# A Mamba, cross-attention and mixture-of-experts decoder on one core: opening, passage to the experts and last norm in another order

## The chip, the core and the metric

The kernel runs on one core of a Trainium2 chip. The time is device microseconds of one execution, and the figure for the kernel before is a median of 3 runs. All arithmetic is float32.

A core has five engines that run their own instruction queues and meet through semaphores: TensorE (PE in the profile; its weight loads are PEld), VectorE (DVE), ScalarE (ACT), GpSimd (POOL) and SyncE (SP). SP only issues DMAs; ACT and POOL issue some of theirs.

## The reference, cut to what matters

Three blocks, each followed by a layernorm: a Mamba layer, an attention over a second sequence, and a mixture of 32 experts with one shared expert. Batch B = 8, length S = 512, width D = 512, inner width 1024, state 16, 16 heads of 32, 4 of 32 experts for each token, capacity 640 rows for each expert.

```python
# Mamba
xz = _layernorm(x, ln_w, ln_b) @ in_proj_w
x_main, z = jnp.split(xz, 2, axis=-1)
x_main = jax.nn.silu(conv1d_causal(x_main) + conv_b)            # 4 taps along the sequence
dt, B_ssm, C_ssm = jnp.split(x_main @ x_proj_w, [DT_RANK, DT_RANK + D_STATE], axis=-1)
dt = jax.nn.softplus(dt @ dt_proj_w + dt_proj_b)
h = dA_t * h + dBx_t                                            # dA = exp(-exp(A_log) * dt), dBx = dt * B * x_main
y_t = jnp.einsum('bdn,bn->bd', h, C_t)                          # for every t of 512
x = _layernorm(x + (res_scale * ((y + x_main * D_param) * jax.nn.silu(z)) @ out_proj_w + x))
# attention over ctx
x = _layernorm(x + softmax(where(mask, q @ k.T / sqrt(32), -1e8)) @ v @ Wo.T + bo)
# experts
scores = softmax(xf @ wg.T)                                     # 8 groups of 4; the best 4 groups, then the best 4 experts
w, idx = top_k(masked, 4);  w = w / (w.sum() + 1e-9)
pos = (jnp.cumsum(oh, axis=0) * oh).sum(-1) - 1;  keep = pos < cap
dest = jnp.where(keep, fe * cap + pos, E * cap)                 # row of the token in its expert's buffer
h = silu(xe @ w1) * (xe @ w3);  out = (h @ w2) * buf_w
y = zeros.at[buf_tok].add(out)
z = silu(xf @ sw1) * (xf @ sw3) @ sw2
out = _layernorm(x + y + z)
```

## The kernel before

The program is three functions, run one after another: `layers()` (Mamba and attention with the gate and the shared expert), `experts()` and `finish()` (the last layernorm). Pools hand out the tiles; a scheduler of the framework may move an instruction within its engine's queue as far as dependencies allow, so the order in the source isn't exactly that on the engines. Line numbers are those of the kernel before.

**Opening of `layers()`.** `const` (L128) allocates a tile and loads it with a DMA on SP. It is called for the layernorm's and convolution's weights, then 16 DMAs bring A_log into `aneg` (L149), ScalarE takes its Exp and VectorE its negative (L153, L154), then come bq, bk, bv, bo and wg, masks and counters on GpSimd, the mask (L217 to L221) which is made into fill values and sent to `filld` in memory, and the load of Wo with four products (L974 to L978) that fold bv through Wo into bo. Only then `load_x` (L272) loads the first 256 rows of x, and `pieces()` (L263) issues the first weights of the Mamba projections. `pieces()` is a generator: it issues one load ahead of the one that it returns, and the tiles `wm` have three buffers.

**First chunk.** `norm_x` computes the layernorm (L54 to L79), `flip_x` transposes (L287), and `convolve` (L303 the projection, L323 the copy, L329 the first tap, L337 the other three) runs for four groups q of 256 channels; each fetches its piece. The tile `xp` has a single buffer. Then `silu` (L354), `x_proj` with `spill` (L360 to L368: B and C go to memory as `scr`), `prepare` (dt for one q: L390 to L413, spread over the partitions by 4 DMAs each for dt and dtx, L419), `bcast` (one group of B and C broadcast from memory, L379) and `decays` (the exponentials with `aneg`, L438).

**The loop.** There are 16 chunks (8 images of two halves of 256 positions), each of 32 steps over (q, g, ci): channel group, group of 4 states, channel block. A step makes h's input (L450), scans (L454), multiplies by C (L471) and sums over states on TensorE (L475). `settle()`, `do()` and `dry()` are a list of deferred second halves: `do` starts a piece of work and leaves its remainder to the next call; `dry` finishes all. Side work is woven into the steps by weights: `sources(0)` in the first image, later `units(b - 1)`, the attention and shared expert of the image before. After the loop, `units(B - 1)` runs alone: flips of x1 (L734), queries (L704 and L743), scores (L767), maxima (L769), and so on to the second layernorm. In chunks 0 and 1, every odd step clears the rows of one expert in the buffer `xbuf` (L237, 1.36 MB).

**Passage to the experts.** The end of `units` is a list built by `add(weight, function)`: transpose x2 (L870), sw1 in four parts, with `pick` (logits L540, the gate L547 to L603) after its first; sw3 in four parts, with `place` (L615 to L636: the position of each token in its expert, counted by matmuls, to `dest`) after the fourth, and after the third for the last image; then 16 `send`s (L642: GpSimd's indirect DMAs that scatter rows to `xbuf`) and the second matmul of the shared expert.

**Pools.** The Mamba tiles lie in the pools `p1`, `p2` and `p3` beside those of the attention; the experts' pools are allocated after `layers()`, and each is tied to the release of what had the space.

**`experts()`.** `load(e)` issues on SP the rows of one expert, `xe` (L1136), and its w1, w3, w2 (L1139, 1 MB each; two buffers), then TensorE flips xe (L1171), VectorE sums weights (L1162: sums of halves of the weights, which take part in the products), and TensorE runs `hidden` (L1200) and the product with w2. GpSimd adds the results into `based` (L1280).

**`finish()`** goes through 8 pieces of 512 rows: load acc on SP (L1367), layernorm on VectorE and ScalarE (helper lines L54 to L79: statistics, Ln and Exp for the root, `m` by five small operations, then four rows o on ScalarE), and a store issued by ScalarE (L1370). acc and o have four buffers each.

Of the kernel before, what the change touches and what calls it, by code (L numbers as in the profile page):

```python
# [1 line left out]

# [5 lines left out]
F32 = mybir.dt.float32  # L8
# [8 lines left out]
P = 128  # L17
# [9 lines left out]
T = 256  # L27
# [54 lines left out]
def layers(ctx, tc, a, x1d, filld, based, xbuf):  # L82
# [23 lines left out]
    nc = tc.nc  # L106
    cp = ctx.enter_context(tc.tile_pool(name="l_const", bufs=1))
# [5 lines left out]
    bcp = ctx.enter_context(tc.tile_pool(name="l_bc", bufs=6))  # L113
# [19 lines left out]

    lnw = const("lnw", [P, DC], a["ln_w"])
# [18 lines left out]
    nc.scalar.activation(aneg, aneg, AF.Exp)  # L153
    nc.vector.tensor_scalar(aneg, aneg, -1.0, None, ALU.mult)  # L154
# [6 lines left out]
    das = [cp.tile([P, NG, T + 1], F32, name=f"l_da{i}") for i in range(2)]  # L161
    for da in das:
        nc.gpsimd.memset(da[:, :, 0:1], 0.0)

    bq = const("bq", [P, DC], a["bq"])
    nc.vector.tensor_scalar(bq, bq, HD**-0.5, None, ALU.mult)
    bk = const("bk", [P, DC], a["bk"])
    bv = const("bv", [P, DC], a["bv"].rearrange("(c p) -> p c", p=P))
    bo = const("bo", [P, D], a["bo"].partition_broadcast(P))
    wg = const("wg", [P, DC, E], rows(a["wg"]))  # L170
# [44 lines left out]

    mu8 = p3.tile([P, D], F32, tag="row", name="mu8").bitcast(U8)[0:B, 0:S]
    nc.sync.dma_start(mu8, a["mask"])  # L217
    fl = p3.tile([P, D], F32, tag="row", name="fl")
    nc.vector.tensor_copy(fl[0:B, :], mu8)
    nc.vector.tensor_scalar(fl[0:B, :], fl[0:B, :], -1.0, 1e8, ALU.add, ALU.mult)  # L220
    nc.sync.dma_start(filld, fl[0:B, :])  # L221

# [21 lines left out]
    def pieces():  # L244


        w_in, w_out = rows(a["in_proj_w"]), rows(a["out_proj_w"])
        xs = [w_in[:, :, 2 * q * P : 2 * (q + 1) * P] for q in range(CC // 2)]
        zs = [w_in[:, :, DI + 2 * q * P : DI + 2 * (q + 1) * P] for q in range(CC // 2)]
        outs = [w_out[:, 2 * q : 2 * q + 2, :] for q in range(CC // 2)]  # L250
        n = B * (S // T)
        order = list(xs)
        for i in range(n):
            order += (outs if i else []) + zs + (xs if i + 1 < n else [])
        order += outs
        got = None
        for src in order + [None]:
            nxt = None
            if src is not None:
                nxt = p2.tile([P, 4 * 2 * P], F32, tag="wm", name="wm", bufs=3).rearrange(  # L260
                    "p (c f) -> p c f", c=src.shape[1]
                )
                nc.sync.dma_start(nxt, src)  # L263
            if got is not None:
                yield got
            got = nxt

    piece = pieces()

    def load_x(b, t, f):  # L270
        f["xt"] = xt = p1.tile([P, NT_, D], F32, tag="xt", name="xt")
        nc.sync.dma_start(xt, a["x"][b, t * T : (t + 1) * T, :].rearrange("(j p) d -> p j d", p=P))  # L272
# [6 lines left out]
    def flip_x(q, f):  # L279
        if q == 0:  # L280
            f["xnT"], f["xs"] = p1.tile([P, DC, T], F32, tag="xnT", name="xnT"), {}
# [30 lines left out]
    def convolve(t, q, f):  # L312
# [4 lines left out]
        def first_tap():  # L317
            xp = p1.tile([P, 2, T + 3], F32, tag="xp", name="xp")
# [7 lines left out]
            f["xs"][q] = xs = p2.tile([P, 2, T], F32, tag="xs", name="xs", bufs=5)  # L326
# [18 lines left out]
    def gate_x(q, f):  # L345
        if q == 0:
            f["zs"] = p1.tile([P, CC, T], F32, tag="zs", name="zs")
        ps = project(f, "ps_z")
        return lambda: nc.scalar.copy(f["zs"][:, 2 * q : 2 * q + 2, :], ps) and None
# [7 lines left out]
    def x_proj(f):  # L357
# [6 lines left out]
        def spill():  # L364
            f["xd"] = xd = p1.tile([64, T], F32, tag="xd", name="xd")
# [19 lines left out]
    def prepare(q, f):  # L385
# [8 lines left out]
        def exponentials():  # L394
            u = p1.tile([P, 2, T], F32, tag="u", name="u")
            dt = p1.tile([P, 2, T], F32, tag="dt", name="dt")
# [6 lines left out]
            l = p1.tile([P, 2, T + 3], F32, tag="xp", name="l")[:, :, 0:T]  # L403
            nc.scalar.activation(l, u, AF.Ln, bias=1.0)
            w = dtx = p1.tile([P, 2, T], F32, tag="dtx", name="dtx")
            nc.scalar.activation(w, u, AF.Identity, bias=1.0)

            def both():
# [6 lines left out]
                for src in (dt, dtx):  # L415
                    to = p2.tile([P, 2, 2, T], F32, tag=f"both{len(f['ready', q])}", name="both")
# [23 lines left out]
    def carry(t, c, g):  # L440

        last = state[:, c, g].unsqueeze(2)
        h = p3.tile([P, NG, T + 1], F32, tag="h", name="h", bufs=4)
# [45 lines left out]
    def twice_x(b, t, f):  # L489
        f["o"] = o = p1.tile([P, NT_, D], F32, tag="xt", name="o")  # L490
# [216 lines left out]
    def units(b):  # L707
# [241 lines left out]
        for j in range(SC):  # L949
            add(0.5, flip2, j, dry=(j == 0))  # L950
        for ic in range(DC):
            add(3.4, hidden, "sw1", ic, dry=(ic == 0))
            if ic == 0:
                add(1.5, lambda: pick(b, st["x2t"], st["x2T"], st))
        for ic in range(DC):
            add(3.4, hidden, "sw3", ic)
            if ic == (2 if b == B - 1 else 3):
                add(0.5, lambda: place(*st["picked"], st))
        sends = [(0, send, j, st) for j in range(SC)]
        if b == B - 1:  # L960
            for part in sends:
                add(*part)
# [5 lines left out]


    load("Wo")  # L970
    rep = p3.tile([P, D], F32, tag="row", name="rep")
    psb = psm.tile([P, D], F32, tag="mm", name="ps_bo")
    for dc in range(DC):
        nc.vector.tensor_copy(rep[:, dc * P : (dc + 1) * P], bv[:, dc : dc + 1].to_broadcast([P, P]))  # L974
        nc.tensor.matmul(
            psb, rep[:, dc * P : (dc + 1) * P], loaded["Wo"][:, dc, :], start=(dc == 0), stop=(dc == DC - 1)
        )
# [442 lines left out]
```

## Time and profile before

| | |
|---|---|
| time, median of 3 runs | 5591.53 us (5585.55 to 5597.78) |
| the profiled execution: its time | 5587.21 us |
| its span on the core | 5585.2 us |
| TensorE busy | 4864.8 us, 87% |
| VectorE busy | 4348.3 us, 78% |
| ScalarE busy | 2589.2 us, 46% |
| GpSimd busy | 565.5 us, 10% |
| mean granted TensorE clock | 0.938 |
| DMA | 769.83 MB, mean 138 GB/s |
| x issued by SP | 26.14 us |
| first product of the scan loop on VectorE | 81.87 us |
| first flips of the last image | 3746.32 us |
| first flips of the first expert | 3969.45 us |
| first statistics of the last norm | 5533.36 us |

The profiled execution is 4.3 us faster than the median. Times in the timelines count from the start of its span. A row has the start, the length, the engine (SPq, ACTq are queues that issue DMAs), the line, the operation, output and inputs by the program's names, and the number of instructions joined in the row; the bracket holds the idle time of the engine before it and what ended that. The rows by stretch give each engine's busy time (and number of instructions), the granted clock of TensorE, the mean busy share of the 16 DMA engines and their rate. The clock is granted in tenths of full speed and says nothing of whether TensorE was busy.

### The profile page before, as it was taken

The page shows a single profiled execution, that of the slowest core. Times are in us where ns is not written, and L with a number is a line of the kernel's source. Part 1 is how long each engine was busy: PE and PEld are TensorE (multiplying, and loading weights), DVE is VectorE, ACT ScalarE, POOL GpSimd, SP SyncE. Part 2 cuts the span into 40 slices and gives each one's busy share as a digit, 9 for nine tenths or more (in the row PEclk, how much of TensorE's full clock was granted, in tenths as well). Part 3 has the DMA queues.
Part 4 walks back from the last instruction along what each step waited for, and adds up shares of the span by engine and source line. Part 5 has one row for each costly group of instructions (what it writes and reads, how often), then busy time and mean ns, then how long its engine had stood idle before and what let it go on. Part 6 is the DMA issues. An engine that isn't in the chain of part 4 may idle for free. (4 is left out here: it accounts for less than half of the span.)

```text
span 5585.2 us, 60354 instructions
## 1 busy us (share of the span) xinstructions
PE 4864.8 (87%) x19752; PEld 2711.8 (49%) x19752; DVE 4348.3 (78%) x5738; ACT 2589.2 (46%) x5481; POOL 565.5 (10%) x424
## 2 busy tenths in 40 slices
PE   5667888888988988888888898889899999999994
PEld 3233344334433434443443343333577777777773
DVE  5998999999889999898989999853566565555554
ACT  4554655565566555565555656523222222222223
POOL 0000002001100200200010020010111111111111
PEclk8778999999999999999999999989999999999997
DMA  7787345444634634543463464431445545454444
GB/s 202 214 230 203 106 130 183 123 115 134 187 105 112 199 103 127 180 129 109 128 199 101 116 189 111 113 118 37 140 124 126 125 125 125 119 126 125 123 115 139
DMA packets 560426, 769.83 MB, mean 138 GB/s; under 512 B 135754, under 2 KB 268394, under 8 KB 560112
## 3 DMA queue, kind: packets, MB, share of 16 engines
q1 hardware_dynamic: 522608, 680.70, 41.6%
q0 software_dynamic: 33280, 76.90, 7.3%
q10 hardware_dynamic: 4224, 8.39, 0.4%
q8 instruction: 156, 2.56, 0.2%
q14 instruction: 158, 1.29, 0.1%
HBM read 508.68 MB, written 165.05 MB: 121 GB/s over the span
## 5 line engine op out<-in xcount | busy, mean ns | idle before, releaser
L438 ACT ACTIVATE l_da<-both,l_aneg 128x256 f32<-128x256 f32 x2048 | 889.1, 499 | 816.9 <-DVE h L454 775.4
L454 DVE TENSOR_TENSOR_SCAN h<-l_da,h 128x1028 f32<-128x1028 f32 x512 | 1169.8, 2292 | 51.6 <-ACT h L444 29.6
L475 PE MATMUL py<-h,l_twice 128*64 128x256 f32 x4096 | 625.4, 419 | 210.5 <-DVE h L471 210.3
L450 DVE TENSOR_TENSOR h<-both,bc 128x1024 f32<-128x1024 f32 x512 | 617.8, 1214 | 134.4 <-PE py L475 72.0
L471 DVE TENSOR_TENSOR h<-h,bc 128x1024 f32<-128x1024 f32 x512 | 622.4, 1218 | 8.2 <-DMA bc<-scr 2.1
L475 PEld LDWEIGHTS py<-h,l_twice 128*64 128x64 f32 x4096 | 292.5, 146 | 585.9 <-DVE h L471 251.0
L767 PE MATMUL ps_s<-l_ka,l_qa 64*128 64x512 f32 x1024 | 319.3, 703 | 141.7 <-DVE mx L769 141.3
L1200 PE MATMUL ps_h<-xT,w 128*128 128x320 f32 x1536 | 436.1, 434 | 0.0
L1280 POOL DMA_INDIRECT based<-y,xe x160 | 252.2, 1577 | 1314.3 <-ACT y L1303 573.8
L769 DVE TENSOR_REDUCE mx<-ps_s 128x2 f32<-128x1024 f32 x256 | 310.1, 1214 | 82.7 <-PE ps_s L767 81.8
L1221 DVE TENSOR_TENSOR hT<-ps_h,p 128x320 f32<-128x320 f32 x128 | 62.9, 491 | 374.9 <-PE ps_h L1200 374.7
L1200 PEld LDWEIGHTS ps_h<-xT,w 128*128 128x128 f32 x1536 | 292.5, 191 | 118.4 <-issue 0.8
L793 PE MATMUL ps_t<-l_qa,l_ka 64*128 64x512 f32 x1024 | 298.0, 646 | 15.8 <-ACT eT L797 12.1
L797 ACT ACTIVATE eT<-ps_t 128x1024 f32<-128x1024 f32 x256 | 258.7, 1012 | 109.5 <-PE ps_t L793 109.3
L809 PE MATMUL po<-eT,l_va 128*64 128x512 f32 x1024 | 279.2, 623 | 24.4 <-ACT raw L821 19.6
L1200 PE MATMUL ps_h<-t,s 128*128 128x320 f32 x1024 | 286.1, 432 | 0.0
L642 POOL DMA_INDIRECT xbuf<-x2t,dest x128 | 218.3, 1706 | 651.2 <-DVE dest L636 561.8
L704 PE MATMUL ps_p<-x2T,wa 128*128 128x512 f32 x512 | 245.5, 629 | 12.9 <-DVE hT L884 10.7
L303 PE MATMUL ps_z<-xnT,wm 128*128 128x256 f32 x1024 | 240.9, 388 | 15.4 <-DVE o L513 13.0
L303 PE MATMUL ps_x<-xnT,wm 128*128 128x256 f32 x1024 | 240.8, 389 | 3.2 <-ACT dt L401 1.9
L504 PE MATMUL po<-wm,zs 128*128 128x512 f32 x512 | 233.3, 605 | 3.3 <-DMA wm<-in_out_proj_w 1.8
L1200 PEld LDWEIGHTS ps_h<-t,s 128*128 128x128 f32 x1024 | 194.6, 190 | 81.1
(225 smaller groups left out, 7401.3 us busy)
## 6 DMA issues: line engine op xcount, KB each, us to landing
bc<-scr SPq DMA_DIRECT2D x1024, 128.0 KB
w<-in_w SPq DMA_DIRECT2D x96, 1024.0 KB
wm<-in_in_proj_w SPq DMA_DIRECT2D x128, 512.0 KB
xbuf<-zero SPq DMA_DIRECT2D x32, 1362.5 KB
xe<-xbuf SPq DMA_DIRECT2D x32, 1362.5 KB
both<-dt SPq DMA_DIRECT2D x256, 128.0 KB
both<-dtx SPq DMA_DIRECT2D x256, 128.0 KB
wm<-in_out_proj_w SPq DMA_DIRECT2D x64, 512.0 KB
```

Of the source, the lines that this page charges most:

```text
L303: nc.tensor.matmul(ps[:, i, :], w[:, dc, i * P : (i + 1) * P], f["xnT"][:, dc, :], start=(dc == 0), stop=(dc == DC - 1),)
L438: nc.scalar.activation(da[:, n, 1:], dt[:, c % 2, j, :], AF.Exp, scale=aneg[:, c, j, g, m : m + 1])
L450: nc.vector.tensor_tensor(steps, dtx[:, c % 2].unsqueeze(2).to_broadcast([P, 2, NG // 2, T]), bc[0], ALU.mult)
L454: nc.vector.tensor_tensor_scan(flat, da.rearrange("p n t -> p (n t)"), flat, 0.0, ALU.mult, ALU.add)
L471: nc.vector.tensor_tensor(steps, steps, bc[1], ALU.mult)
L475: nc.tensor.matmul(py[j * HP : (j + 1) * HP, c % 2, :], twice, h[:, j * 2 + m, 1:], start=False, stop=(s == (NST // NG - 1, NG // 2 - 1, 1)),)
L767: nc.tensor.matmul(ps[:, j, :], qa[r, lt * P : (lt + 1) * P], ka[r, :], start=True, stop=True)
L769: return lambda: nc.vector.tensor_reduce(mx[:, lt, :].unsqueeze(2), ps, AX.X, ALU.max) and None
L793: nc.tensor.matmul(ps[:, j, :], ka[r, kc * P : (kc + 1) * P], qa[r, :], start=True, stop=True)
L797: nc.scalar.activation(eT, ps, AF.Exp)
L809: nc.tensor.matmul(po[j * 2 * HD : (j + 1) * 2 * HD, :], va[:, kc, i, j * HD : (j + 2) * HD], eT[:, j, :], start=(kc == 0), stop=(kc == SC ...
L1200: nc.tensor.matmul(ps, w[:, n, r * P : (r + 1) * P], x[:, n, :], start=not more and n == 0, stop=n == 1, skip_group_check=more,)
```

## The change

It is in six parts, and leaves the arithmetic of every one of them as it was.

- x's first rows are loaded by SP's first instruction, and two pieces of Mamba's weights are started ahead of the constants (`begun`). Aneg's Exp and sign move to just before the first `decays`.
- The bias work (scale of bq, the mask's fill values, Wo and bo) moves into a function, called in the steps k = 0 (load of Wo) and k = 2 of the first chunk; the scheduler places it early in them.
- The clears of chunks 0 and 1 follow a count spread over the 64 steps from step 6 on, in place of every odd step.
- The Mamba tiles go into a pool of their own, `l_mamba`, allocated first together with the pool of bc, so that the experts' constants and weights take the space that it frees. The weights of expert 0 are issued by ACT.
- For the last image only, `pick` comes ahead of sw1, `place` after the first part of sw3, and the sends after the second part.
- `finish` starts the statistics of piece i before it completes piece i − 1, and maps rows as "(p j) d", so that a partition holds 4 rows that follow each other in memory (8 KB in one) instead of 4 separate rows of 2 KB.

The diff, cut:

```diff
+    mp = ctx.enter_context(tc.tile_pool(name="l_mamba", bufs=1))
+    bcp = ctx.enter_context(tc.tile_pool(name="l_bc", bufs=6))
     cp = ctx.enter_context(tc.tile_pool(name="l_const", bufs=1))
...
-    bcp = ctx.enter_context(tc.tile_pool(name="l_bc", bufs=6))
...
+    def begun(it):
+        first = next(it)
+        return chain([first], it)
+
+    x0 = p1.tile([P, NT_, D], F32, tag="xt", name="xt")
+    nc.sync.dma_start(x0, a["x"][0, 0:T, :].rearrange("(j p) d -> p j d", p=P))
+    piece = begun(pieces())
     lnw = const("lnw", [P, DC], a["ln_w"])
...
-    nc.scalar.activation(aneg, aneg, AF.Exp)
-    nc.vector.tensor_scalar(aneg, aneg, -1.0, None, ALU.mult)
+    bq = const("bq", [P, DC], a["bq"])
...
-    bq = const("bq", [P, DC], a["bq"])
-    nc.vector.tensor_scalar(bq, bq, HD**-0.5, None, ALU.mult)
...
-    mu8 = p3.tile([P, D], F32, tag="row", name="mu8").bitcast(U8)[0:B, 0:S]
-    nc.sync.dma_start(mu8, a["mask"])
...
-    nc.sync.dma_start(filld, fl[0:B, :])
...
-    piece = pieces()
...
-        f["xt"] = xt = p1.tile([P, NT_, D], F32, tag="xt", name="xt")
+        f["xt"] = xt = mp.tile([P, NT_, D], F32, tag="xt", name="xt")
...
+        end = b == B - 1
+        if end:
+            add(1.5, lambda: pick(b, st["x2t"], st["x2T"], st), dry=True)
+        sends = [(0, send, j, st) for j in range(SC)]
         for ic in range(DC):
             add(3.4, hidden, "sw1", ic, dry=(ic == 0))
-            if ic == 0:
+            if ic == 0 and not end:
                 add(1.5, lambda: pick(b, st["x2t"], st["x2T"], st))
         for ic in range(DC):
             add(3.4, hidden, "sw3", ic)
-            if ic == (2 if b == B - 1 else 3):
+            if ic == (0 if end else 3):
                 add(0.5, lambda: place(*st["picked"], st))
-        sends = [(0, send, j, st) for j in range(SC)]
-        if b == B - 1:
-            for part in sends:
-                add(*part)
+            if ic == 1 and end:
+                for part in sends:
+                    add(*part)
...
-    f = {}
-    load_x(0, 0, f)
+    f = {"xt": x0}
...
     bc, n = bcast(f, 0), 0
+    nc.scalar.activation(aneg, aneg, AF.Exp)
+    nc.vector.tensor_scalar(aneg, aneg, -1.0, None, ALU.mult)
     decays(0, 0, f["ready", 0][0], das[0])
...
+            if i == 0 and k == 0:
+                load("Wo")
+            if i == 0 and k == 2:
+                biases()
...
-            if i < 2 and k % 2:
-                clear(i * E // 2 + k // 2)
+            while i < 2 and cleared < E * (i * len(steps) + k - 6) // (2 * len(steps) - 7):
+                clear(cleared)
+                cleared += 1
...
+        start = nc.sync.dma_start if e else nc.scalar.dma_start
         nc.sync.dma_start(xe, xbuf[e * CAP : (e + 1) * CAP, :].rearrange("(j p) d -> p j d", p=P))
         for n in ("w1", "w3", "w2"):
             got[n] = w = wp.tile([P, DC, D], F32, tag=n, name=n)
-            nc.sync.dma_start(w, a[n][e].rearrange("(c p) f -> p c f", p=P))
+            start(w, a[n][e].rearrange("(c p) f -> p c f", p=P))
...
+    def sums(i):
         rows = slice(i * S, (i + 1) * S)
         acc = pp.tile([P, SC, D], F32, tag="acc", name="acc")
-        nc.sync.dma_start(acc, based[rows, :].rearrange("(j p) d -> p j d", p=P))
+        nc.sync.dma_start(acc, based[rows, :].rearrange("(p j) d -> p j d", j=SC))
...
+            nc.vector.bn_stats(st, acc[:, j, :])
+            nc.vector.bn_aggr(mv[:, j, :], st)
...
+        nc.scalar.activation(r, v, AF.Ln)
+        nc.scalar.activation(r, r, AF.Exp, scale=-0.5)
+        return rows, acc, mv, v, r
...
+    def end(rows, acc, mv, v, r):
...
+        for j in range(SC):
+            nc.scalar.activation(o[:, j, :], acc[:, j, :], AF.Identity, bias=m[:, j : j + 1], scale=r[:, j : j + 1])
+        nc.scalar.dma_start(out[rows, :].rearrange("(p j) d -> p j d", j=SC), o)
...
+    for i in range(B):
+        now = sums(i)
+        if last:
+            end(*last)
+        last = now
+    end(*last)
```

`biases()` holds the lines that were at L166, L217 to L221 and L975 to L978 unchanged; in `finish`, `end(*last)` holds the five small operations of the helper and the four rows on ScalarE. All other tiles of the Mamba chunk (`wm`, `xnT`, `xp`, `xs`, `zs`, `xd`, `u`, `dt`, `l`, `dtx`, `both`, `h`, `l_da`, `o`) move to `mp` with the number of buffers that they had.

## The prediction

> **What bounds the kernel now.** I read the page's busy shares and slices first (TensorE 87% busy over the whole span, VectorE 78%), then busy time by stretch, then the timelines of the stretches where neither engine works.
>
> ```profile
> start us, us, engine line op out<-in xcount [idle before <-releaser]
> 26.14 0.39 SPq L272 DMA_DIRECT2D xt<-in_x  x1
> ...
> 31.79 1.29 DVE L73 BATCH_NORM_STATS2 st<-xt 128x6 f32<-128x512 f32 x2 [5.49 <-DMA xt<-in_x]
> ...
> 81.87 2.36 DVE L450 TENSOR_TENSOR h<-both,bc 128x1024 f32<-128x1024 f32 x2 [8.16 <-DMA bc<-scr]
> ```
>
> Opening: SP sends x at 26.14, behind every constant; the first work of the scan loop is at 81.87.
>
> ```profile
> core 0: us, PE busy (x) PEld busy (x) DVE busy (x) ACT busy (x) POOL busy (x), PEclk, DMA share, GB/s
> 82.00:300.00 218.00, 145.82 (x614) 76.39 (x615) 209.77 (x213) 114.75 (x275) 12.90 (x4) 0.80 0.73 210
> 3739.00:3766.00 27.00, 19.01 (x44) 8.86 (x46) 0.13 (x1) 5.25 (x8) 0.13 (x1) 0.75 0.24 73
> 3950.00:3976.00 26.00, 4.20 (x16) 3.03 (x17) 6.19 (x10) 0.00 (x0) 6.14 (x7) 0.54 0.77 284
> 4100.00:5508.00 1408.00, 1407.98 (x5764) 1040.86 (x5762) 827.49 (x1487) 389.71 (x851) 231.99 (x147) 1.00 0.48 118
> 5540.00:5545.00 5.00, 0.00 (x0) 0.00 (x0) 4.96 (x15) 2.66 (x7) 0.00 (x0) 0.50 0.30 61
> ```
>
> The loop is VectorE's (209.77 of 218); in the experts TensorE never pauses. Time can therefore come only from the seams: to 82, at 3739 to 3766, at 3950 to 3976, and after 5523. The last image:
>
> ```profile
> 3746.32 1.94 PE L734 MATMUL ps_tr<-l_ident,xr 128*128 128x128 f32 x8 [9.13 <-DMA xr<-x1d]
> ...
> 3766.60 3.68 DVE L769 TENSOR_REDUCE mx<-ps_s 128x2 f32<-128x1024 f32 x3 [27.46 <-PE ps_s L767]
> ...
> 3909.28 0.29 DVE L547 TENSOR_REDUCE g_m<-ps_l 128x4 f32<-128x128 f32 x1 [15.49 <-PE ps_l L540]
> ...
> 3929.76 0.39 PE L615 MATMUL ps_b<-g_any,l_before 128*128 128x128 f32 x2
> ...
> 3956.99 0.97 POOL L642 DMA_INDIRECT xbuf<-x2t,dest  x1 [0.30 <-issue]
> ...
> 3969.45 1.09 PE L1171 MATMUL ps_t<-e_ident,xe 128*128 128x128 f32 x4 [21.31 <-DMA xe<-xbuf]
> ```
>
> and the finish:
>
> ```profile
> 5527.88 27.58 SPq L1367 DMA_DIRECT2D acc<-based  x8
> 5533.36 1.29 DVE L73 BATCH_NORM_STATS2 st<-acc 128x6 f32<-128x512 f32 x2 [26.28 <-DMA acc<-based]
> ...
> 5545.43 0.15 DVE L59 TENSOR_TENSOR m<-v,r 128x4 f32<-128x4 f32 x1
> ...
> 5580.15 0.38 ACTq L1370 DMA_DIRECT2D out<-o  x1
> ```
>
> Read the bracket as the engine's idle time before, and what ended it.
>
> **The change part by part.**
>
> **1. Opening.** In before, 26.14 to 59.52 (the end of the last taps on VectorE) is x, statistics, flips, four projections. Now x is SP's first DMA with two pieces of weights behind it, and the constants follow. x took 5.65 us from issue to first use (31.79 − 26.14), so the statistics start near 6 instead of 31.8, and the first two groups of taps are done before 22. The third piece is new trouble: it sits on SP behind all the constants. SP's last constant issue was at 24.14; x and two pieces now stand in front (1.7 by their issue rows)[...], while mask and Wo have left the place (I take +2.3 in all), so it goes out near 26.4 and lands near 30.6: 4.2 us, an estimate between bc's 2.98 us for 128 KB (78.89 to 81.87) and the 5.62 us of w1's 1 MB (3959.84 to 3965.46). Now TensorE has stood idle some 11 us. The timeline and the granted clock do not agree about what that costs:
>
> ```profile
> 27.00:30.00 3.00, 0.11 (x1) 0.14 (x1) 0.00 (x0) 0.00 (x0) 0.00 (x0) 1.00 0.94 307
> ...
> 29.89 5.48 PE L975 MATMUL ps_bo<-wa,rep 128*128 128x512 f32 x8 [29.89 <-DMA wa<-in_Wo]
> ```
>
> By the clock column (1.00) the restart is free: 16 matmuls are 3.5 us. But these eight took 0.685 us each, where the warm ones in the queries' row (32 in 16.53) average 0.52. [...] 5.3 us for the third projection. Taps at 35.9; the last group 4.3 us behind (the pace before was 4.14): 40.2 + 0.6 copy + 0.6 first tap + 2.7 = 44.2, against 59.52: **15.3 sooner** (by the clock column 17.1). Off this come: the bias work, now inside the first step, its mask, filld and Wo DMAs behind pieces 3 to 5 on SP (the add that took 0.69 at 35.41 sits between dtx L409 and l L410 and waits for ps_bo, 8 matmuls queued behind ps_dt: 0.7 to 2.9, I take 1.3), and bc now wholly behind both issues on SP (0.65). Aneg's Exp and −1 (0.31 + 0.23) move behind the silus on ACT, hidden while the spread of dt lands. **13.4** (10 to 17), first h product near 68.5.
>
> **2. Clears and the first chunks.** The 32 clears of 1.36 MB are spread: 4 instead of 6 before the first scan, 28 instead of 26 in two chunks of loop. No path waits for a clear itself; what they can delay is a bc, both or wm behind them on SP. In the loop 82 to 520 VectorE's waits for DMA sum to bc 8.2 (all at the start, before the first product) and xt 4.7, so I take 0 (−5 to +5). Cover gone: 3.4 us of transfer each (1.36 MB at the 409 GB/s that the finish moves). Later in the loop instructions keep their order.
>
> **3. Weights beside the last image.** Mamba's tiles now end with the loop and their space holds the weights of experts 0 and 1, 6.3 MB, whose DMAs go out at about 3743: expert 0's on ACT as soon as x1d's store has read the tile that they overwrite, expert 1's on SP behind xr. They meet xr (four DMAs at 3743.55), qa's spreads and the mask. The row says DMA share 0.24, so the room is there, and by it alone: 0. [...] I take flips 2.4 later, **−2.4** (0 to −6), since xr is on the path (9.13 idle, released by xr). Behind it also: 16 sums of weights on VectorE (0.66 each, 10.6 us) are queued ahead of mx, in 27.46 us of idle; and qa's spreads stand behind 3 MB on SP, landing near 3764.5 where ps_s needs them at 3767.8.
>
> **4. Gate.** Logits moved in front of sw1: ps_l was done at 3909.24; 32 small matmuls after x2T at 3899.9, cold, end near 3905. The gate on VectorE (3909.28 to 3923.1, 13.5 us) then ends at 3918.4. On TensorE sw1 (32 × 0.43) and one quarter of sw3 follow from 3905 to 3922.1, and ps_b stands behind: 3922.1 against 3929.76, 7.7 sooner. Next in the queue is the silu of hT and one product on VectorE (3923.5), ahead of the location: dest at 3927.8 against 3935.05, **7.2**. The 16 sends take 1.28 each as before; xe then goes out first where w1 was (0.6), and without w1's 1 MB in front of it (2.57 at 408 GB/s, I take 2.5). Behind xe everything is there. **10.3** (7 to 13). What is late next: the path is xe's landing, some 7 us after issue; the shared experts' matmuls are covered, as TensorE was 21.31 us idle before the flips.
>
> **5. Finish.** In before m of piece 2 (5545.43) stood on VectorE behind the statistics of pieces 3 and 4, ACT idled to 5546.51, out 2 went at 5549.47, and load 6 waited for its buffer. I walked the three queues with the row durations (statistics 0.60 each, aggregate 0.08, ACT 0.72 a row, 2.57 us a MB shared[...]): it gives 5585.9 where the span ends at 5585.2. The new order gives outs at 5543.2, 5547.7, 5555.5, 5560.4, 5564.2, 5569.0, 5572.6, 5575.2 and an end at 5580.3: **5.6** (2 to 8). The new wait: out 3 stands on ACT behind the first row of o 4, which needs the statistics of load 5. Rows of 8 KB in place of 2 KB: no row of the trace shows them; the 2 KB rate is already 409 GB/s, so 0, −2 to +2.
>
> Sum: 13.4 − 2.4 + 10.3 + 5.6 = 26.9. The profiled execution took 5587.21 (span 5585.2 and 2.0 around it), 4.3 under the median of 5591.53. So 5560.3 against it; the median's kin is 5564.6.
>
> **The rivals.**
>
> A. The seams give half. The third piece is later still [...], the bias add waits the full 2.9, and xr comes 5 later: 9 − 5 + 8.5 + 3 = 15.5, so 5576. For: SP spends 24 us on constants in any order. Against: nothing else is between piece and taps.
>
> B. The finish gains nothing: loads and stores together are 16.8 MB, 41 us at 409 GB/s, out of the 52 us from 5533 to 5585; if the smooth order runs the DMA full, only 2 remain. Then 23.3: 5568. Against: the stretch 5540 to 5545 moved 61 GB/s.
>
> C. Slower: the clears. 28 of them are now laid evenly between the bc DMAs of chunks 0 and 1, and DMA is at 0.73 there. If each keeps the next bc waiting by more than 1 us beyond VectorE's cover, 28 × 1 eats 26.9; at the whole 3.4 it costs 95, and the result is 5660. It decides from 1 us a clear. Against: before had one at every odd step, 26 in the same stretch, with 8.2 us of waiting for bc in all.
>
> D. The weights don't come early: if space is freed only with the pool's other tiles, experts' weights come after the last image, and part 3 is 0, xe has w1 beside it: 13.4 + 7.8 + 5.6 = 26.8: the same time.
>
> **How the numbers follow.** My forecast has 0.6, A 0.22, B (alone) 0.08, D 0.04, C 0.06. The forecast's own bounds (10 to 17, −6 to 0, 7 to 13, 2 to 8, clears ±5) are half-widths of 3.5, 3, 3, 3 and 5, in quadrature 8, and the median of the runs itself has some ±4 (they span 5585.55 to 5597.78): ±9 around 5564.6. The range reaches past A's 5576 and down by as much: 5550 to 5579. A measurement of this kernel tells about 0.2% (11 us) from no change: faster by that needs under 5580. Forecast, B and D are there, A nearly always: 0.91; within 0.2%: 0.05 (A's tail, half of C); slower: 0.04.
>
> **What would show it.** Right: first statistics before 8 us, a gap on TensorE between the second and third ps_x of about 10 us, the first h product at 66 to 72; in the last image, the flips 9 us after the norm instead of 7, and the weights' DMAs on ACT and SP beside them; the gate's dest some 7 us nearer to the last x2T copy; the first expert's flips about 32 us after dest instead of 34.4; the last out 52 us after the last put instead of 57.2. Wrong: bc among VectorE's waits in the first two chunks (C), a VectorE idle before mx longer than 30 (part 3 worse), or DMA slices in the finish still with gaps (part 5).

## The result and the profile after

| | before | after |
|---|---|---|
| time, median of 5 runs | 5591.53 us (5585.55 to 5597.78) | 5566.23 us (5558.27 to 5569.36) |
| ratio | | 0.9951, 95% interval 0.9940 to 0.9962 |
| profiled execution, span | 5585.2 | 5567.7 |

The median fell by 25.3 us where 26.9 was forecast. The kernel before was run twice more beside the changed one, which left its median where it was; the quotient of the two medians is 0.9955. The two profiled executions differ by 17.5 only: executions of one kernel lie up to 12 us apart in these ten, and the profiled one of after was the slowest of its five. So I read the gain by stages, each between two instructions that both traces have.

The opening, from the timeline of the kernel after (columns as before: start, length, engine, line, operation, output and inputs, count, and in the bracket the idle time before and what ended it):

```profile
5.05 1.29 DVE L74 BATCH_NORM_STATS2 st<-xt 128x6 f32<-128x512 f32 x2 [5.05 <-DMA xt<-in_x]
...
27.66 1.57 SPq L156 DMA_DIRECT2D wm<-in_in_proj_w  x3
...
31.65 9.90 PE L302 MATMUL ps_x<-xnT,wm 128*128 128x256 f32 x32 [10.08 <-DMA wm<-in_in_proj_w]
...
69.93 2.36 DVE L449 TENSOR_TENSOR h<-both,bc 128x1024 f32<-128x1024 f32 x2 [9.14 <-DMA bc<-scr]
```

x is worked on at 5.05 us instead of 31.79. The third piece of weights goes out behind the constants at 27.66, and TensorE stands 10.08 us for it. First product at 69.93, before at 81.87.

The last image's start and its gate:

```profile
3738.37 1.09 PE L733 MATMUL ps_tr<-l_ident,xr 128*128 128x128 f32 x4 [9.14 <-DMA xr<-x1d]
3740.95 1.09 PE L733 MATMUL ps_tr<-l_ident,xr 128*128 128x128 f32 x4 [1.50 <-DMA xr<-x1d]
...
3892.73 7.04 PE L539 MATMUL ps_l<-l_wg,x2T 128*128 128x32 f32 x32
3899.59 19.86 PE L703 MATMUL ps_p<-x2T,wa 128*128 128x512 f32 x40
3919.28 0.39 PE L614 MATMUL ps_b<-g_any,l_before 128*128 128x128 f32 x2
...
3956.69 1.08 PE L1191 MATMUL ps_t<-e_ident,xe 128*128 128x128 f32 x4 [11.75 <-DMA xe<-xbuf]
```

The flips come in two halves with a wait of 1.50 us between them. The logits took 7.04 us. In the kernel before they stand behind eight wide matmuls, and took 3.65:

```profile
3899.92 5.83 PE L704 MATMUL ps_p<-x2T,wa 128*128 128x512 f32 x8 [0.68 <-ACT x2T L871]
3905.59 3.65 PE L540 MATMUL ps_l<-l_wg,x2T 128*128 128x32 f32 x32
```

The first expert starts at 3956.69, before at 3969.45.

The finish:

```profile
5517.08 29.33 SPq L1390 DMA_DIRECT2D acc<-based  x8
5521.90 1.29 DVE L1394 BATCH_NORM_STATS2 st<-acc 128x6 f32<-128x512 f32 x2 [26.04 <-DMA acc<-based]
...
5527.43 0.13 DVE L1405 TENSOR_TENSOR m<-v,r 128x4 f32<-128x4 f32 x1
...
5539.13 1.29 DVE L1394 BATCH_NORM_STATS2 st<-acc 128x6 f32<-128x512 f32 x2 [3.79 <-DMA acc<-based]
...
5543.04 0.81 ACT L1412 ACTIVATE o<-acc,m,r 128x512 f32<-128x512 f32 x1 [0.65 <-DVE m L1409]
5543.05 0.34 ACTq L1413 DMA_DIRECT2D out<-o  x1
...
5562.94 0.34 ACTq L1413 DMA_DIRECT2D out<-o  x1
```

The last store goes out 41.0 us after the first statistics (before 46.8). The wait that is left is the one forecast: the third store (5543.05) stands behind the first row of the fourth piece on ScalarE, and that piece's m behind the statistics of the fifth, whose load waited for a buffer (VectorE idle 3.79 us).

### The profile page after: what moved, and what is told of

The parts are those of the page before. It is cut to its first block, busy times and chain, and to the rows that moved or that the text cites. A ratio compares the mean times of both kernels' runs of the same rounds, so it can differ in the third digit from the quotient of the medians.

```text
span 5567.7 us, 60361 instructions
## 1 busy us (share of the span) xinstructions
PE 4880.6 (88%) x19752; PEld 2718.5 (49%) x19752; DVE 4349.5 (78%) x5738; ACT 2592.1 (47%) x5481; POOL 569.2 (10%) x424
## 5 line engine op out<-in xcount | busy, mean ns | idle before, releaser
L792 PE MATMUL ps_t<-l_qa,l_ka 64*128 64x512 f32 x1024 | 299.6, 648 | 20.9 <-ACT eT L796 17.5
L796 ACT ACTIVATE eT<-ps_t 128x1024 f32<-128x1024 f32 x256 | 259.1, 1013 | 110.1 <-PE ps_t L792 109.6
L703 PE MATMUL ps_p<-x2T,wa 128*128 128x512 f32 x512 | 243.9, 625 | 11.8 <-DVE hT L883 10.3
```

The source lines that it names most:

```text
L792: nc.tensor.matmul(ps[:, j, :], ka[r, kc * P : (kc + 1) * P], qa[r, :], start=True, stop=True)
L796: nc.scalar.activation(eT, ps, AF.Exp)
```

## The stages of all profiled executions

All times in us, from the timelines of each run's one profiled execution. The marks are: first product of the loop (h from both and bc); the last layernorm of Mamba on ScalarE (o from o and less, last image); the first mx of the last image; its last x2T copy; the last dest; the first expert's first flips; the last put; the end of the span.

| run | to first product | loop | norm to mx | mx to x2T | x2T to dest | dest to flips | flips to last put | put to end |
|---|---|---|---|---|---|---|---|---|
| before | 81.87 | 3657.30 | 27.43 | 132.68 | 35.77 | 34.40 | 1553.50 | 62.25 |
| after | 69.93 | 3661.28 | 29.01 | 132.73 | 32.03 | 31.71 | 1555.27 | 55.74 |
| e_gate | 81.42 | 3672.20 | 26.40 | 131.62 | 32.13 | 34.94 | 1554.09 | 62.40 |
| e_finish | 83.06 | 3659.73 | 26.36 | 129.53 | 35.09 | 34.93 | 1553.37 | 55.43 |
| e_rows | 69.30 | 3665.18 | 29.06 | 132.56 | 31.99 | 31.56 | 1553.12 | 57.73 |
| e_pools | 67.81 | 3654.36 | 26.32 | 129.75 | 31.36 | 37.80 | 1553.75 | 55.45 |
| e_clears | 68.57 | 3659.50 | 28.77 | 131.92 | 31.98 | 31.69 | 1552.84 | 56.03 |
| f_pick | 68.39 | 3665.81 | 28.71 | 131.29 | 29.34 | 31.59 | 1554.35 | 55.82 |
| f_late | 55.13 | 3672.07 | 28.98 | 129.79 | 31.60 | 31.87 | 1554.66 | 55.20 |
| f_wlate | 69.62 | 3659.31 | 27.47 | 132.73 | 32.15 | 32.44 | 1553.62 | 55.46 |
| f_fin8 | 68.75 | 3668.23 | 28.83 | 132.60 | 32.10 | 31.66 | 1553.74 | 53.19 |
| f_best | 53.22 | 3664.37 | 28.83 | 129.79 | 28.95 | 31.74 | 1553.90 | 52.70 |

The columns fall into groups by the edit that a run has. Within a group, x2T to dest, dest to flips and put to end repeat within 1 us, norm to mx and the first product within about 1 and 2. Mx to x2T (129.5 to 132.7) and flips to last put (1552.8 to 1555.3) vary by some 3 us whatever the edit, and the loop by 18, 3654 to 3672. With that scatter, two single executions or two medians of a few runs can't settle parts of 3 us each; the stages can.

## The experiments

**e_gate: the kernel before with part 4 alone.**

```diff
+        if end:
+            add(1.5, lambda: pick(b, st["x2t"], st["x2T"], st), dry=True)
...
-            if ic == (2 if b == B - 1 else 3):
+            if ic == (0 if end else 3):
```

> The kernel before with part 4 alone (for the last image the logits ahead of sw1, the location after the first part of sw3, the sends after the second). Theory (from the two traces): the logits' matmuls of 32 columns run at half clock and leave it there, so they take 7.0 us instead of 3.65 and the first part of sw1 behind them is as slow as before (6.0 against 5.8); from the last x2T copy to dest 32.0 us (before 35.8), the time 3.7 lower: about 5587.8 against a median of 5591.5. The prediction's own step: [...] dest 28.6 us after the copy, 7.2 lower: 5584.3. Rival: the gain seen in the changed kernel's trace came from elsewhere (the moved pools), so that dest stays 35 to 36 us after the copy. From dest to the first flips 34.4 as before under all.

Measured: x2T to dest 32.13, as in the kernel after; dest to flips 34.94. So the gate's new order alone gives the gain that the changed kernel shows there (3.5 in the mean of all runs with it), half of the 7.2 forecast. The time is 5586.04 against 5588.57, ratio 0.9995 (0.9986 to 1.0004): 3.6 us can't be told from nothing in whole runs, as the loop of its profiled execution (3672.20) shows.

**f_pick: the logits behind the first part of sw1 again, the rest of the changed kernel kept.**

```diff
-        if end:
-            add(1.5, lambda: pick(b, st["x2t"], st["x2T"], st), dry=True)
...
-            if ic == 0 and not end:
+            if ic == 0:
```

> The changed kernel with one edit: for the last image the logits stand behind the first part of sw1 again (8 wide matmuls), the rest of part 4 stays. Theory: the 32 narrow matmuls do not count as work for the clock, the 8 wide ones do. So the logits run at full clock (3.65 us instead of 7.0), the rest of sw1 too, and the gate on VectorE, no longer TensorE, ends last: ps_b some 23.7 us after the last x2T copy instead of 26.3, dest 29.3 instead of 32.0; time 2.7 below the changed kernel's. Rival: the logits are slow for another reason (their weight loads fill the engine whatever the clock), and ps_b stays at 26 or comes later, since the logits start 6 us later: dest 32 or more.

Measured: ps_b 23.64 after the copy, dest 29.34, both as the theory has them to 0.1. The timeline, first:

```profile
3894.84 5.86 PE L703 MATMUL ps_p<-x2T,wa 128*128 128x512 f32 x8 [0.68 <-ACT x2T L870]
3900.53 3.65 PE L539 MATMUL ps_l<-l_wg,x2T 128*128 128x32 f32 x32
3904.03 13.98 PE L703 MATMUL ps_p<-x2T,wa 128*128 128x512 f32 x32
3917.84 0.38 PE L614 MATMUL ps_b<-g_any,l_before 128*128 128x128 f32 x2
```

and the rows by stretch that tell why: of f_pick,

```profile
3894.00:3897.00 3.00, 2.32 (x4) 1.14 (x4) 0.00 (x0) 0.59 (x1) 0.00 (x0) 0.50 0.00 0
3897.00:3900.00 3.00, 3.00 (x5) 1.10 (x5) 0.00 (x0) 0.00 (x0) 0.00 (x0) 0.63 0.00 0
3900.00:3904.00 4.00, 4.00 (x34) 3.65 (x33) 0.00 (x0) 0.59 (x1) 0.00 (x0) 1.00 0.00 0
```

and of the changed kernel:

```profile
3893.00:3896.00 3.00, 3.00 (x16) 3.00 (x16) 0.00 (x0) 0.54 (x1) 0.00 (x0) 0.50 0.00 0
3896.00:3900.00 4.00, 4.00 (x19) 4.00 (x20) 0.19 (x1) 0.00 (x0) 0.00 (x0) 0.50 0.00 0
3900.00:3903.00 3.00, 3.00 (x4) 1.07 (x4) 2.45 (x9) 0.31 (x1) 0.00 (x0) 0.50 0.01 3
3903.00:3906.00 3.00, 3.00 (x7) 1.26 (x6) 2.69 (x10) 0.25 (x1) 0.00 (x0) 0.75 0.00 0
```

The clock is the third number from the end. Seven us of logits, with TensorE and its weight loads busy all the time, left it at 0.50; the wide matmuls behind them had to raise it, as they have to where they stand first. All twelve traces agree. In the eight with the logits in front, these took 7.03 or 7.04 us, and the clock rose (by rows of 0.1 us) 3.6 to 5.2 us after the first wide matmul; in the four with eight wide matmuls ahead (before, e_finish, f_pick, f_best), the logits took 3.65 or 3.66, and the clock rose 2.9 to 4.4 us after the first wide one. So the logits gave no start: in front they ran at half clock (7.04 us in the changed kernel, 3.65 in f_pick), and what followed started at half clock too (its 40 wide matmuls took 19.86 us, f_pick's 8 and 32 took 5.86 and 13.98). Whether it is their 32 columns that don't count, or the share of the time that their weight loads take, no run separates. The gain of f_pick over the changed kernel in the stage is 2.7 us; in the time (5565.96 against 5566.23, of different sets of runs) it can't be seen.

**e_finish and e_rows: the finish alone, and the finish with its old rows.** e_finish is the kernel before with the new `finish`; e_rows is the changed kernel with

```diff
-        nc.sync.dma_start(acc, based[rows, :].rearrange("(p j) d -> p j d", j=SC))
+        nc.sync.dma_start(acc, based[rows, :].rearrange("(j p) d -> p j d", p=P))
...
-        nc.scalar.dma_start(out[rows, :].rearrange("(p j) d -> p j d", j=SC), o)
+        nc.scalar.dma_start(out[rows, :].rearrange("(j p) d -> p j d", p=P), o)
```

> The kernel before with part 5 alone (statistics one piece in front, 8 KB rows). Theory: from the last put to the end of the span 55.7 us instead of 62.25, the time 6.5 lower: about 5585. Rival: part of the finish's gain came from the state that the changed kernel left (other pools, other DMA in flight), then 58 or more from last put to end.

> The changed kernel with the old rows in the finish (four rows of 2 KB per partition instead of 8 KB in one). Theory: the order gives the gain, the layout nothing, since both move 400 GB/s: from the last put to the end 55.7, within 1. Rival: the layout gives it: 58 to 62, time 2 to 6 us above the changed kernel's. A third case: first statistics later by the 0.5 us by which the changed kernel's came sooner (9.94 against 10.41 after the last put), and the rest equal: 56.2.

Measured: 55.43 with the new finish on the kernel before, 57.73 with the old rows in the changed one. The order gives 4.6 of the 6.7 us (62.3 to 57.7), the layout, of loads and stores together, 2.1 (57.7 to 55.6, the mean of the runs with both): the forecast had 5.6 and 0. Of the 2.1 some 0.8 lies ahead of the first statistics (10.72 us after the last put, against 9.94 in the changed kernel). In the stretch rows the last number is GB/s. The changed kernel (8 KB), then e_rows (2 KB):

```profile
5540.00:5545.00 5.00, 0.00 (x0) 0.00 (x0) 3.70 (x15) 2.16 (x5) 0.00 (x0) 0.50 1.01 428
```

```profile
5540.00:5545.00 5.00, 0.00 (x0) 0.00 (x0) 3.50 (x13) 0.20 (x1) 0.00 (x0) 0.50 1.05 409
```

In time e_finish has 5581.90 against 5588.57, ratio 0.9990 (0.9982 to 0.9999); e_rows 5567.42, which can't be told from the changed kernel.

**f_fin8: eight buffers for acc.**

```diff
-        acc = pp.tile([P, SC, D], F32, tag="acc", name="acc")
+        acc = pp.tile([P, SC, D], F32, tag="acc", name="acc", bufs=8)
```

> The changed kernel with eight buffers for acc in the finish instead of four. Theory: loads 5 to 8 wait for a buffer (the five us from 5530 on moved 103 GB/s between stretches of 430), so with a buffer each all of them go at once: from the last put to the end 47 us (10 to the first statistics, 16.8 MB at 428 GB/s less what lies before it, and the last piece's rows) instead of 55.7. Rival: loads ahead of the stores only push the stores back, and ScalarE's rows (8 times 2.9 us from the first m on) and the last store set the end: 53 or more.

Measured: 53.19, 2.4 better and not the 8.7 of the theory: the rival held. All loads go out in 7.56 us, but the statistics of the pieces that land early now stand in front of the m of earlier ones on VectorE:

```profile
5541.60 0.81 ACT L1412 ACTIVATE o<-acc,m,r 128x512 f32<-128x512 f32 x1 [2.16 <-DVE m L1409]
...
5547.89 0.81 ACT L1412 ACTIVATE o<-acc,m,r 128x512 f32<-128x512 f32 x1 [3.17 <-DVE m L1409]
```

and behind these ScalarE has four more pieces of rows to do, with one more wait of 1.47 us, to the end. Taking away the wait for a buffer brought back, in part, the wait that the change had removed.

**e_pools: the Mamba tiles in the shared pool again.** `mp` is `p1`, and bcp is allocated in its old place; ACT still issues expert 0's weights.

> The changed kernel with part 3's pools undone (Mamba's tiles in the pool of the others again, so that the first experts' weights come only after the last image; expert 0's still go out on ACT). Theory: the last image is undisturbed (norm's rows to the last x2T copy 160.1 us as before, against 161.7), but w1 shares the DMA engines with xe, so that the first flips come 34 us after dest instead of 31.7: net 0.7 us slower than the changed kernel. Rival: xr's delay isn't from the weights, and the last image stays 161.7. Second rival: without early weights their sums on VectorE come into the path: the first ps_h more than 8 us after the first flips (6.6 in both kernels).

Measured: norm to mx 26.32 as in the three runs of the old pools (26.4 to 27.4), against 28.9 in the mean of the seven with early weights. Dest to flips 37.80 against 31.7, worse than in the kernel before (34.8): xe is issued 25.2 us after dest, as in the changed kernel, but the flips follow 12.6 us after the issue instead of 6.5, with three loads of 1 MB on ACT beside it. The lines of e_pools: the flips of the last image undivided, and the first expert's weights going out just ahead of xe.

```profile
3729.29 1.94 PE L732 MATMUL ps_tr<-l_ident,xr 128*128 128x128 f32 x8 [9.10 <-DMA xr<-x1d]
3731.91 15.45 PE L702 MATMUL ps_p<-x1T,wa 128*128 128x512 f32 x32 [0.68 <-ACT x1T L733]
...
3934.34 1.56 ACTq L1158 DMA_DIRECT2D w<-in_w  x3
...
3934.81 0.91 SPq L1155 DMA_DIRECT2D xe<-xbuf  x2
...
3947.40 1.09 PE L1190 MATMUL ps_t<-e_ident,xe 128*128 128x128 f32 x4 [17.84 <-DMA xe<-xbuf]
```

Part 3 thus costs up to 2.3 (f_wlate puts it at 1.9) and gives 3.1 against the kernel before. The expectation of 34 for this run was wrong: it took w1 alone to share with xe, and there were three loads. The time, 5566.50, is that of the changed kernel.

**f_wlate: the weights in between.**

```diff
-            start(w, a[n][e].rearrange("(c p) f -> p c f", p=P))
+            d = start(w, a[n][e].rearrange("(c p) f -> p c f", p=P))
+            if e < 2:
+                tc.keep_in_program_order(d)
```

> The changed kernel with the weights of experts 0 and 1 kept behind the last image's work in their queues (expert 0's on ACT after its last instruction there, about 30 us before xe; expert 1's on SP behind xe). Theory: it is the sharing of the DMA engines with xr that costs the last image 2.6 us before mx (29.0 against 26.4 where the weights come late) and up to 5 in all (161.7 against 156 to 160), and sharing with xe that costs 6 where the weights come late (37.8 against 31.7); in between there is room. So norm's rows to mx 26.4, dest to first flips 31.7 or less, and 2 to 5 below the changed kernel. Rival: the weights' sums (10.6 us of VectorE) then lie in the way of the gate or of the first flips: dest later by some us, or first ps_h more than 8 us after the first flips.

Measured: norm to mx 27.47, dest to flips 32.44: 1.5 won back and 0.7 lost, less than expected. But the wait for xr is gone altogether. The flips are undivided, and the queries begin 9.73 us after the norm's rows, as in the four runs with the old pools (9.74 to 9.81), against 11.3 to 12.2 in the seven with early weights, whose mean is 1.9 later:

```profile
3736.05 1.94 PE L733 MATMUL ps_tr<-l_ident,xr 128*128 128x128 f32 x8 [9.10 <-DMA xr<-x1d]
3738.66 16.60 PE L703 MATMUL ps_p<-x1T,wa 128*128 128x512 f32 x32 [0.67 <-ACT x1T L734]
```

So the early weights cost 1.9 us. The rest of the differences in norm to mx is the clock's: the 32 query matmuls took 16.60 us here and 15.45 in e_pools, because the clock rose 5.3 us after the first of them here and 3.0 us there. In all twelve traces it rose after 2.9 to 5.3 us, early weights or not. The sums stood in nobody's way (first ps_h 6.6 us after the flips). The rest of the last image (mx to x2T) was 132.7, and varies from 129.5 to 132.7 in all runs with no regard to the weights, so the "up to 5" of the expectation was no effect of part 3. Time 5567.22: no difference.

**f_late: three pieces ahead, the late constants behind the fourth.**

```diff
     def begun(it):
-        first = next(it)
-        return chain([first], it)
+        first = [next(it), next(it)]
+        return chain(first, it)
...
     for q in range(CC // 2):
         do(convolve, 0, q, f, first=(q == 0))
+        if q == 2:
+            late()
```

with the loads of A_log, bq, bk, bv, bo, wg, the ones rows and the zero rows in `late()`.

> The changed kernel with another order on SP in the opening: three pieces of weights ahead of the constants instead of two, and A_log, the biases, the ones rows and the zero rows behind the fourth piece. Theory: the third piece behind the constants is what the opening still waits for (TensorE idle 10.1 us before it, then 6.6 us for its 16 matmuls at half clock instead of 3.5): all four groups of taps then follow at the pace of 4.14 us, the last ends near 34.6 instead of 46.3, and the first h product is at 58 instead of 69.9; time 11 to 12 below the changed kernel's. Rival: SP is then busy with the constants until 37 us and scr, Wo and bc queue behind them, or aneg comes late for the decays: first product at 63 or later.

```profile
12.13 15.85 PE L310 MATMUL ps_x<-xnT,wm 128*128 128x256 f32 x64 [0.26 <-ACT xnT L299]
...
55.13 2.36 DVE L457 TENSOR_TENSOR h<-both,bc 128x1024 f32<-128x1024 f32 x2 [3.14 <-DMA both<-dtx]
```

Measured: the four projections run through, and the first product is at 55.13, 14.8 sooner than in the changed kernel, 3 more than expected. But the first chunk is longer: from the first product to the first store of x1d 211.2 us, against 203 to 206 in all others but f_best (209.8). VectorE was busy 202.7 us between 55 and 267, against 199.8 between 70 and 274 in the changed kernel (the layernorm of the second chunk's x, for one, ran in the opening's idle time there), and waited in places such as

```profile
189.74 2.36 DVE L457 TENSOR_TENSOR h<-both,bc 128x1024 f32<-128x1024 f32 x2 [3.49 <-DMA bc<-scr]
```

where two clears stand between the bc issues on SP. So about half is given back. Time 5559.39, ratio to before 0.9936 (0.9919 to 0.9952).

**e_clears: the clears at every odd step again.** The `while` of part 2 is replaced by the old two lines.

> The changed kernel with the clears at every odd step of chunks 0 and 1 again (part 2 undone). Theory: the clears' places cost nothing in either order: first product to x1d's first store 204, to the second 395, within 2, and the first product at 68 to 70. The prediction's rival C: the new spacing makes bc late, so that with the old one chunks 0 and 1 are shorter by several us (second store at 390 or less). The other way: six clears instead of four before the first scan delay bc, and the first product is 2 to 6 us later.

Measured: first product at 68.57; first and second store of x1d 205.9 and 395.8 after it (changed kernel 204.2 and 395.3). Part 2 costs and gives nothing that can be told. Time 5562.40, ratio 0.9950 (0.9934 to 0.9965).

**f_best: f_late, f_pick and f_fin8 together.**

> The changed kernel with the three edits together that gained in their stages: the opening's constants behind the pieces, the logits behind the first part of sw1, eight buffers for acc. If the stages add: first h product at 55, the first chunk some 8 us longer than in the changed kernel (x1d's first store 211 us after the first product instead of 204), dest 29.3 us after the last x2T copy, last put to end 53.2: 7 + 2.7 + 2.5, together about 12 below the changed kernel's 5566, so 5554 and a ratio of 0.993 to the kernel before. If they don't (the first chunk's order comes out differently again), 5556 to 5566.

Measured: 5549.50 us (5545.27 to 5554.83), ratio to the kernel before 0.9929 (0.9916 to 0.9943). First product 53.22, first chunk 209.8, dest 28.95 after the copy, last put to end 52.70: the stages add. e_clears, which is the changed kernel but for the clears and ran in the same set, has 5562.40, so 12.9 more, where about 12 was forecast. All five of its times lie below all five of the changed kernel (from 5558.27) and all four of e_clears (from 5561.53); the intervals of the ratios to before overlap by 0.0003.

## Why the prediction was right

The mechanisms forecast held in all parts but one, the gate; that the total came so near is partly luck. Summed by stages, in means over the runs that have each part and those that don't: opening 82.1 to 68.9, 13.2; norm to mx −2.3; x2T to dest 35.4 to 31.9, 3.5; dest to flips 34.8 to 31.7, 3.1; finish 6.7. That is 24.2, and the medians differ by 25.3; the 1.1 between belong to no stage, and lie within the scatter of the medians.

- **Opening, 13.4 forecast, 13.2 measured** in means of seven and three traces (11.9 in the two profiled executions of the result). No run undoes the opening alone. The mechanism was as told, down to the idle TensorE between the second and third group (10.08, "some 11"). In the terms there were offsets: the third piece went out at 27.66 and not 26.4 (SP's issues of the constants cb and w_dt took 1.84 and 1.46 us, 0.58 each in the kernel before; what held them the profile doesn't name), and its 16 matmuls took 6.6 us (31.65 to the copy at 38.26), not 5.3, so the last taps ended at 46.3 instead of 44.2. The bias add found ps_bo ready and cost 0.68 instead of 1.3. The scheduler had moved aneg's Exp (23.96) and the fill values (42.06) far ahead of their places in the source, between the taps, whose groups kept their pace of 4.14. Of durations and column, the durations were right: in the stretch from 31 to 34 the clock column, which said 1.00 at the restart in the kernel before (27 to 30 there), says 0.50. How long that would last was, in the 5.3, the author's estimate; no trace of before showed it. Here the clock rose at 37.2, 5.6 us after the first of the 16. Ahead of its fall to 0.50 (at 27.0) the column can't be read: the first two rows below both say 1.00, for matmuls of 0.37 us and of 0.22. (The 0.52 that the prediction calls warm is a mean over a start at half clock, 5.1 of the 16.53 us; behind the logits in f_pick, at 1.00, 32 of the same shape took 13.98, 0.44 each.)

```profile
13.00:16.00 3.00, 3.00 (x8) 2.37 (x8) 0.00 (x0) 0.00 (x0) 0.00 (x0) 1.00 0.39 6
16.00:21.00 5.00, 5.00 (x23) 4.30 (x23) 1.51 (x4) 1.68 (x3) 0.19 (x1) 1.00 0.39 6
26.00:31.00 5.00, 0.00 (x0) 0.00 (x0) 0.53 (x3) 0.00 (x0) 0.12 (x1) 0.60 0.56 180
31.00:34.00 3.00, 2.35 (x6) 1.93 (x7) 0.00 (x0) 0.00 (x0) 0.00 (x0) 0.50 1.01 313
```

- **Clears, 0 forecast, 0 measured** (e_clears). The prediction's reading of before, bc waits "all at the start", missed one of 2.1 us at 490.4; the changed kernel has one of 1.9 at 259.1, e_clears one of 1.4. So rival C's mechanism is there once in either order, and decides nothing; f_late shows it larger (3.49) when the loop's order shifts.
- **Weights beside the last image, −2.4 forecast, −2.3 measured**, where the row of DMA share (0.24) alone would have given 0; the 2.4 was the author's estimate. Shown by e_pools and f_wlate: 1.9 us is the wait for xr, the rest the chance of the clock, which rose 2.9 to 5.3 us after the first query matmul. The forecast's sign, flips 9 us after the norm instead of 7, came for the second half only: the first four came at 7.2 as before, the other four at 9.7. The sums on VectorE stayed in its idle time.
- **Gate: the step that failed.** "7.7 sooner" for ps_b came out as 4.1 (3.9 by means). The forecast let the logits end near 3905, 5.7 us, and sw1 follow at 0.43 us a matmul. The logits took 7.04 us and ended 6.8 after the copy, 1.1 later than forecast. The 40 wide matmuls behind them took 19.86 us instead of 17.2, 2.7 more, since the first of them still ran at half clock (0.50 in the row 3900 to 3903). That the logits would bring the clock up was the author's estimate, which no trace of before showed. In the runs, matmuls of 512 columns raised it, 2.9 to 5.3 us after the first, and those of 32 did not in 7.0 us. f_pick's forecast, made with that difference, had 29.3 us from the copy to dest, and 29.34 was measured.
- **Xe without w1 in front of it, 3.1 forecast, 3.1 measured.** Of the two terms the 0.6 for going out first was hardly there (25.4 us after dest before, 25.3 after). The flips came 9.0 us after xe's issue before and 6.5 after, so 2.5 sooner, as forecast for w1's 1 MB. First the kernel before, then the changed one:

```profile
3959.84 0.38 SPq L1139 DMA_DIRECT2D w<-in_w  x1
3960.45 0.37 SPq L1136 DMA_DIRECT2D xe<-xbuf  x1
```

```profile
3950.24 0.89 SPq L1156 DMA_DIRECT2D xe<-xbuf  x2
```

- **Finish, 5.6 forecast, 6.7 measured.** The order gave 4.6, a little less than the walk of the queues; the 8 KB rows, put at 0 within ±2 because no row of the trace showed them, gave 2.1. One of the signs of being wrong showed too: the finish still has a gap in its DMA (22 GB/s from 5530 to 5533), while loads wait for buffers.

The errors, −3.7 at the gate, +1.1 in the finish, and small ones, partly cancel, so the time fitted better than its parts. Of the rivals, A had the opening (9), xr (−5) and the finish (3) too low; for the gate and xe together its 8.5 was nearer to the 6.6 measured than the forecast's 10.3. B was wrong: the finish gained 6.7, not 2 (e_finish). D did not happen: the weights went out at 3735.78. The time could not have told D from the forecast, since both put it within 0.1 us.

Open: what makes the loop's length differ by up to 18 us from one execution to another. It starts in the third chunk (store of x1d 636 to 650 us after the first product), and TensorE's granted clock in the stretch 460 to 700 is 0.95 in the shortest loop and 0.91 in the longest; f_best, with 0.96, has one of 3664, so the clock there is not all of it, and no run varied it by itself.

## What to carry to other kernels

Where a kernel has one bound engine throughout, order changes pay at its seams, and the length of a seam can repeat within one or two us, even when whole executions scatter by ten: measure there. Before moving small matmuls to the front of a stage that starts with an idle TensorE, ask what will raise its clock: here 7.0 us of matmuls of 32 columns left it at 0.50. And a wait that is removed by reordering (m behind other pieces' statistics) can come back when the data come sooner, as in f_fin8 (2.16 and 3.17 us on ScalarE), unless the order itself is fixed.

## What was not expected of the hardware

Thirty-two matmuls of 32 columns, with TensorE busy for 7.0 us, left the granted clock at 0.50; matmuls of 512 columns raised it 2.9 to 5.3 us after the first. Transfers with 8 KB in one piece in each partition moved 428 GB/s where rows of 2 KB moved 409 (5540 to 5545 in the changed kernel and in e_rows). In the opening the clock column reads 1.00 before TensorE has done anything: in the kernel after, 13.0 to 16.0 holds eight matmuls of 0.37 us at 1.00, close to the 0.39 of the six at 0.50 (31 to 34), while 16 to 21 has 0.22. In the traces of before and after the column could be trusted only after its first change.
